# A graph attention layer on one core: more row buffers in the setup, self loops ahead of their states, stores moved in the round order

## The chip, the cores and the metric

The kernel runs on one core of a Trainium2 chip. The metric is device microseconds of one launch, from the first instruction to the last. The engines are named as in the profile: PE (matrix multiplies) with its weight loads PEld, DVE (vector), ACT (scalar, activation functions), POOL (the general engine, which here issues the gathers), and SP, which only issues transfers; SPq is SP's queue.

## The reference

12,500 nodes with 128 features, 400,000 edges sorted by destination, 32 features on an edge. One layer of a graph network:

```python
h   = relu(layernorm(x))
xl  = ln1(h) @ W_l ; xr = ln1(h) @ W_r          # 8 heads of 16
# every edge, and one self loop for each node with the mean edge feature
m   = leaky_relu(xl[src] + xr[dst] + ea @ W_e, 0.2)
a   = softmax over the edges of one dst of sum_c m[., h, c] * att[h, c]
g   = sum over the edges of one dst of a * xl[src] + bias
h2  = h + g
out = x + h2 + gelu(ln2(h2) @ W1 + b1) @ W2 + b2
```

## The kernel before, in words

**Setup (lines 704 to 745).** The 98 tiles of 128 nodes are taken in 25 quads. A loop over "rounds" r runs software-pipelined stages, each some rounds later than the one before: statistics of x on DVE (x_stats, L470), ReLU (L481) and squares (L506) on ACT, transposes and the product with W_l on PE, and x_l (L526) on DVE, which writes the row of 136 numbers that edges will fetch; x_l goes out to memory by SP (L534). x_l writes into one of only three tiles (L513), so the fourth x_l waits until the store of the first has landed.

In the same loop POOL fetches, by 24 x 4 indirect transfers (raw_gather, L268 to L276), rows of x for 24 of the 782 edge pairs; SP stores each group to memory three rounds later (raw_store, L279). The groups go through a ring of buffers (L269). The list rows_at (L719) says in which round a group is fetched. Three lumps of work stand in the loop too: edge_constants (L346, round 7, 22 operations on DVE), from_first (L387, round 12, which turns each edge's destination into a distance from the first one of its unit, and of its pair, with two big subtractions on POOL, L392, stored by SP, L398), and fits (L400, round 14, DVE, whose result `flag` decides which branch runs). At the end all engines go on to the branch; its pools begin with small memsets (POOL L876, DVE L878).

**Edge rounds (lines 1320 to 1339).** The 400,000 edges are 782 pairs of two units of 256 edges. One round handles a different pair in every stage; the number beside a stage is how many rounds after the pair's own round it runs. gather (-4) lets POOL issue four indirect transfers that fetch 128 rows each (L897); for the 24 prepared pairs it is one SP transfer instead (L892). windows (-3) lets SP load edge features and distances for four pairs (L908, L914) and the pair's window of xr (L918). place (-1, DVE L925) makes the one-hot matrix. combine (0, PE L939 to L943), slope (ACT L949) and bend (DVE L954) (1), score (2, PE L960, L961), lowest (DVE L968) and weigh (ACT L979) (3), turn (4, PE L987), keep_turned (5, ACT L992), collect (6, PE L1001), own_heads (7, DVE L1010, L1016), put (8, SP L1023, which writes a running state for the pair's nodes, one of two state arrays per unit). The ring of gathered rows has 12 buffers (L862): the gather of pair c needs the collect of pair c-12 to be over. Within an engine everything runs in the order of the program, and the order within a round is written by hand in the list `stages` (L1251), then `steps`, then `late_stages` (L1265), where windows and put stand.

**Node groups.** 25 groups of up to four node tiles are finished between the edge rounds when their edges are over. A group starts at its "round" and its 20 steps run in the offsets of the list `steps` (L1276): f_load (loads of both states, of xl and of xr, L1060), the self loop (f_order, f_z, f_bend, f_score, offsets 1 to 4), the softmax over two states and the self loop (f_low to f_h), the second norm, the two products with GELU between, and f_store (L1242), which adds three terms on DVE and issues the store of the result from SP in the same step (L1249). The last group starts at round 790, eight rounds after the last pair's own round. Groups start at least GAP = 23 rounds apart.

Of the kernel before, what the change touches and what calls it, by code (L numbers as in the profile page):

```python
# [13 lines left out]
F32 = mybir.dt.float32  # L14
BF16 = mybir.dt.bfloat16
I32 = mybir.dt.int32
AF = mybir.ActivationFunctionType
OP = mybir.AluOpType
# [3 lines left out]
P = 128  # L22
# [11 lines left out]
KU = 2  # L34
U = KU * P
UP = 2
QP = 4
RU = 14
# [10 lines left out]
AHEAD = 4  # L49
# [86 lines left out]
def tile_gnn(  # L136
# [23 lines left out]
    nc = tc.nc  # L160
# [8 lines left out]
    RP = -(-NU // RU)  # L169
    assert NU * U <= NCH * CE <= RP * RU * U  # L170
    x_t = x.rearrange("(t p) f -> p t f", p=P)
    out_t = out.rearrange("(t p) f -> p t f", p=P)
# [9 lines left out]
    dc_dram = dram.tile([RP * RU * U], BF16, name="dc_dram")  # L182
    du_dram = dram.tile([RP * RU * U], BF16, name="du_dram")
    raw = [{"c": c, "i": i, "round": r, "n": UP * KU} for i, (c, r) in enumerate(raw_pairs(NT, n_edges))]
# [36 lines left out]
    rng = pre.enter_context(tc.tile_pool(name="rng", bufs=1))  # L221
    node = pre.enter_context(tc.tile_pool(name="node", bufs=3))
# [8 lines left out]
    EP = RU * U  # L231
# [34 lines left out]
        )  # L266

    def raw_gather(d):  # L268
        d["x"] = node.tile([P, UP * KU, P], F32, name="raw", bufs=5)  # L269
        for j in range(d["n"]):  # L270
            nc.gpsimd.indirect_dma_start(  # L271
                out=d["x"][:, j, :],
                out_offset=None,
                in_=x,
                in_offset=bass.IndirectOffsetOnAxis(ap=src_raw[:, d["i"], j : j + 1], axis=0),
            )  # L276
# [97 lines left out]

    df = rng.tile([RP, EP + U + 1], F32, name="df")
    bad = rng.tile([RP, 2], F32, name="bad")

    def last_of_units():
        nc.vector.tensor_copy(lu, dc[:, U - 1 : EP : U])

        u = NUE - 1
        nc.sync.dma_start(
            lu[u // RU : u // RU + 1, u % RU : u % RU + 1],
            bass.AP(tensor=dst.tensor, offset=dst.offset + n_edges - 1, ap=[[0, 1], [1, 1]]),
        )

    def from_first():  # L387
        nc.vector.tensor_copy(df, dc)
        for step, to in ((U, du_dram), (UP * U, dc_dram)):
            de = df[:, 0:EP].rearrange("p (u e) -> p u e", e=step)  # L390
            dlb = rng.tile([RP, EP], BF16, name="dlb", bufs=2)
            nc.gpsimd.tensor_tensor(  # L392
                dlb.rearrange("p (u e) -> p u e", e=step),
                de,
                de[:, :, 0:1].to_broadcast([RP, EP // step, step]),
                op=OP.subtract,
            )
            nc.sync.dma_start(to.rearrange("(p e) -> p e", e=EP), dlb)  # L398

    def fits():  # L400
# [301 lines left out]
    LAST = 8  # L702
    first_xr = xr_steps(node, lambda: once_ps.tile([P, GN * P], F32, name="w_ps"))
    with tc.manual_schedule():
        make_identity(nc, ident)
        count_up()
        for t in xls:
            nc.gpsimd.memset(t[:, :, P:], 1.0)
        load_weights()
        load_x(0, min(GN, NT))  # L710
        load_raw()
        load_x(GN, min(3 * GN, NT - GN))
        for t in range(4 * GN, NT, 14):
            load_x(t, min(14, NT - t))
        load_dst()
        load_consts()
        nc.gpsimd.memset(empty, 0.0)
        nc.gpsimd.memset(empty[:, :, C + 1 : SH], CAP)
        rows_at = [i * 5 // 4 + (3 if i >= 10 else 0) for i in range(len(raw))]  # L719
        for r in range(max(max(len(qs), 9) + LAST + 1, rows_at[-1] + 4)):  # L720
            for d, at in zip(raw, rows_at):
                if r == at:
                    raw_gather(d)
                if r == at + 3:
                    raw_store(d)
            if r == 3:
                weights()
            if r == 7:
                edge_constants()
            if r == 8:  # L730
                last_of_units()
            if r == 12:
                from_first()
            if r == 14:
                fits()
            for t in slots(r - 2):
                nc.vector.reciprocal(t, t)
            for t in slots(r - 1):
                nc.scalar.activation(t, t, AF.Sqrt)
            for late, f in node_stages:  # L740
                if 0 <= r - late < len(qs):
                    f(qs[r - late], r)
            if 0 <= r - LAST < len(first_xr):
                first_xr[r - LAST](qs[0])
        clear(0)
# [82 lines left out]
def window_edges(  # L828
# [9 lines left out]
    nc = tc.nc  # L838
# [20 lines left out]
    with ExitStack() as es:  # L859
# [192 lines left out]
        def tiles(name, d, tag=None, bufs=1):  # L1052
            d[name] = fin.tile([P, GN, P], F32, name=f"f_{name}", tag=tag or f"f_{name}", bufs=bufs)
            return d[name][:, 0 : d["n"]]
# [2 lines left out]
            d[name] = ps2.tile([P, EPR], F32, name=ring)  # L1057
            return d[name]

        def f_load(d):  # L1060
            n, ts = d["n"], d["ts"]
            d["st"] = fin.tile([P, 2, GN, SW], F32, name="st", tag="big", bufs=3)
            for i in range(2):
                nc.sync.dma_start(d["st"][:, i, 0:n], state[i].rearrange("(t p h) f -> p t (h f)", p=P, h=H)[:, ts, :])
            d["xl"] = fin.tile([P, GN, XW], F32, name="f_xl")
            nc.sync.dma_start(d["xl"][:, 0:n], xl_t[:, ts, :])
            d["xr"] = fin.tile([P, GN, NS, P], BF16, name="f_xr")
            nc.sync.dma_start(d["xr"][:, 0:n], xs_t[:, ts, :, :])
# [137 lines left out]
        def f_up(k):  # L1206
            def up(d):
                n, u = d["n"], bank_of(d, f"u{k}")
                nc.tensor.matmul(  # L1209
                    u[:, 0 : n * P],  # L1210
                    w1_sb[:, k * P : (k + 1) * P],
                    d["hT"][:, 0:n].rearrange("p t f -> p (t f)"),
                    start=True,
                    stop=True,
                )

            return up

        def f_gelu(k):
            def gelu(d):  # L1220
                n = d["n"]
                if k == 0:
                    d["gel"] = fin.tile([P, 2, GN * P], F32, name="gel", tag="big", bufs=3)
                nc.scalar.activation(
                    d["gel"][:, k, 0 : n * P], d[f"u{k}"][:, 0 : n * P], AF.Gelu, bias=cols[:, 5 + k : 6 + k]
                )

            return gelu
# [12 lines left out]

        def f_store(d):  # L1242
            n = d["n"]
            y = tiles("yo", d, "f_b")
            up = d["y"][:, 0 : n * P].rearrange("p (t f) -> p t f", f=P)
            nc.vector.tensor_add(up, up, d["x"][:, 0:n])
            nc.vector.tensor_add(up, up, h_sb[:, d["ts"], :])
            nc.vector.tensor_add(y, up, b2_r[:, None, :].to_broadcast([P, n, P]))  # L1248
            nc.sync.dma_start(out_t[:, d["ts"], :], y)  # L1249

        stages = (  # L1251
            (-AHEAD, gather),
# [11 lines left out]
        )  # L1264
        late_stages = (  # L1265
            (-WAHEAD, windows),
            (LATE + 2, put),
        )
        sum_stages = (
            (0, sum_load),  # L1270
# [1 line left out]
            (3, mean),  # L1272
        )
        SUM_STEP = 2
        early = ((17, f_gelu(1)),)
        steps = (  # L1276
            (0, f_load),
            (1, f_order),
            (2, f_z),
            (3, f_bend),  # L1280
            (4, f_score),
            (5, f_low),
            (6, f_exp),
            (7, f_den),
            (8, f_out),
            (9, f_h),
            (10, f_stats),
            (11, f_root),
            (12, f_scale),
            (13, f_turn),  # L1290
            (14, f_turned),
            (15, f_up(0)),
            (16, f_up(1)),
            (16, f_gelu(0)),
            (18, f_down),
            (19, f_store),
        )
        GAP = 23
        last_round = n_pr + LATE + 2
        free = SUM_STEP * (NL - 1) + 5  # L1300
        for d, u in zip(groups, done_after(NT, n_edges)):
            d["round"] = max(free, (u // UP if u < NUE else n_pr) + LATE + 2)
            free = d["round"] + GAP
# [14 lines left out]

        CLEAR = 8
        with tc.manual_schedule():  # L1320
            for r in range(-AHEAD, max(last_round, groups[-1]["round"] + 20)):
                in_round(r, early)
                for late, f in stages:
                    c = r - late
                    if 0 <= c < n_pr:
                        f(c)
                for late, f in sum_stages:
                    i, off = divmod(r - late, SUM_STEP)
                    if off == 0 and 0 <= i < NL:
                        f(i)  # L1330
                if r > 0 and r % CLEAR == 0 and r // CLEAR < NT // GT:
                    clear(r // CLEAR)
                in_round(r, steps)
                in_round(r, enumerate(xr_steps), qs[1:])
                in_round(r, enumerate(raw_steps), raw)
                for late, f in late_stages:
                    c = r - late
                    if 0 <= c < n_pr:
                        f(c)
# [358 lines left out]
```

## Time and profile before

| what | value |
|---|---|
| median of three runs | 4033.95 us (4027.9 to 4034.51) |
| the profiled execution | 4031.16 us, span of its records 4029.0 us, clock granted 0.954 |
| busy: PE, DVE, ACT, POOL | 3542.0, 2539.1, 2131.2, 2980.9 us |
| instructions: PE, DVE, ACT, POOL | 19059, 5835, 4638, 3155 |
| chain that ended last, by engine | PE 38%, POOL 25%, DMA 22%, issue 13% |
| transfers | 560.85 MB, 139 GB/s in the mean |

A profile gives, for one execution, each engine's busy time and the groups of instructions with their mean duration and the idle time just before them, with the releaser: what ended that idle time. The timeline lists instructions in order: start, duration, engine, line, operation, and in square brackets the idle time before it and its releaser. A row can stand for several instructions in a stretch (x2, x13); its duration is then that of the stretch, waits included. "issue" is time in which the engine waited for nothing that is shown. A transfer's row on SPq is its issue; when it lands is seen only from what waits for it. The profiled execution's 4031.16 us is 2.16 us more than its span; the median of the runs is 2.8 us above the profiled execution.

### The profile page before, as it was taken

Reading aid. Unit: us, or ns where it says so; the run is one execution under the profiler, and the core shown is the slowest. Engines: PE = TensorE matmul, PEld = TensorE weight load, DVE = VectorE, ACT = ScalarE, POOL = GpSimd, SP = SyncE. Lnnn points to the kernel's source line nnn. Section 1 sums busy time; section 2 is a strip of 40 time slices with the busy share of each in tenths; the row PEclk is TensorE's granted clock in tenths of the full one; section 3 lists DMA queues with packets and bytes.
Section 4 is the critical chain, followed back from the end, with each engine's and each line's share of the span. In section 5 each row is a group of like instructions: output and inputs, shape, how many; then the busy total and the mean of one; then the engine's idle time right before and its main releaser. Section 6 shows DMA issues by size and latency. Waiting matters only on the chain.

```text
span 4029.0 us, 65580 instructions
## 1 busy us (share of the span) xinstructions
PE 3542.0 (88%) x19059; PEld 2507.7 (62%) x19255; DVE 2539.1 (63%) x5835; ACT 2131.2 (53%) x4638; POOL 2980.9 (74%) x3155
## 2 busy tenths in 40 slices
PE   3488888888899999999999999989999999989986
PEld 2356666666666666666666666666666666666664
DVE  6556666666666666666666666666666665656654
ACT  5544544544455555555465456555555555545553
POOL 6777777777777777777777777777777777777772
PEclk7799999999999999999999999999999999999998
DMA  6778878767666666656666666656666666566562
GB/s 185 207 175 192 193 184 190 174 160 168 164 120 137 124 124 132 125 112 131 131 126 131 126 132 124 128 127 115 124 136 126 125 131 130 111 131 112 120 133 56
DMA packets 646655, 560.85 MB, mean 139 GB/s; under 512 B 384830, under 2 KB 523949, under 8 KB 646045
## 3 DMA queue, kind: packets, MB, share of 16 engines
q1 hardware_dynamic: 545709, 339.00, 33.7%
q0 software_dynamic: 100000, 217.41, 30.4%
q8 instruction: 156, 2.56, 0.3%
q14 instruction: 214, 1.75, 0.2%
q10 hardware_dynamic: 576, 0.13, 0.0%
HBM read 489.80 MB, written 66.32 MB: 138 GB/s over the span
## 4 chain that ended last, share of the span: by engine, by line
PE 38%; POOL 25%; DMA 22%; issue 13%; SPq 1%; DVE 1%; ACT 0%; POOLq 0%; DVEq 0%; ACTq 0%
POOL xs L897 23%; DMA xs<-xl_dram,src_sb 21%; PE z L943 8%; PE acc L1001 8%; PE ab L961 7%; PE pt_ps L987 4%; PE z L939 4%; PE z L942 2%; POOL raw L271 2%; PE ab L960 1%; PE acc L1234 1%; PE acc L1209 1%; SPq L283 0%; DMA state<-rec 0%; DMA dc<-in_dst 0%
## 5 line engine op out<-in xcount | busy, mean ns | idle before, releaser
L897 POOL DMA_INDIRECT xs<-xl_dram,src_sb x3029 | 2868.9, 947 | 923.3 <-issue 792.7
L979 ACT ACTIVATE p<-ab,rec 128x256 f32<-128x256 f32 x1563 | 655.5, 471 | 1055.2 <-DVE rec L968 1039.1
L1010 DVE TENSOR_TENSOR own<-acc,diag 128x272 f32<-128x272 f32 x782 | 343.6, 439 | 1049.5 <-PE acc L1001 1034.9
L1001 PE MATMUL acc<-xs,pt 128*128 128x136 f32 x6250 | 879.8, 285 | 0.2 <-DVE f_yo L1248 0.2
L939 PE MATMUL z<-ident,xs 128*128 128x128 f32 x3125 | 562.6, 283 | 349.9 <-DMA xs<-xl_dram,src_sb 319.2
L939 PEld LDWEIGHTS z<-ident,xs 128*128 128x128 f32 x3125 | 398.7, 142 | 756.6 <-DMA xs<-xl_dram,src_sb 419.8
L943 PE MATMUL z<-ea,we_z 128*128 128x512 f32 x1564 | 839.4, 619 | 0.1
L961 PE MATMUL ab<-m,negrep 128*128 128x512 f32 x1564 | 799.5, 593 | 11.0 <-issue 1.1
L1001 PEld LDWEIGHTS acc<-xs,pt 128*128 128x128 f32 x6250 | 807.1, 196 | 0.4 <-PE pt_ps L987 0.4
L992 ACT COPY pt<-pt_ps 128x512 f32<-128x512 f32 x782 | 455.1, 582 | 619.5 <-PE pt_ps L987 613.8
L987 PEld LDWEIGHTS pt_ps<-ident,p 128*128 128x128 f32 x3125 | 408.6, 146 | 440.8 <-issue 391.2
L968 DVE TENSOR_REDUCE rec<-ab 128x2 f32<-128x512 f32 x781 | 539.7, 691 | 121.8 <-PE ab L961 113.3
L954 DVE TENSOR_TENSOR m<-z,zs 128x512 f32<-128x512 f32 x782 | 532.6, 681 | 127.4 <-ACT zs L949 127.0
L949 ACT ACTIVATE zs<-z 128x512 f32<-128x512 f32 x782 | 472.6, 604 | 41.1 <-DMA ea<-in_ea_t 32.2
L987 PE MATMUL pt_ps<-ident,p 128*128 128x128 f32 x3125 | 490.2, 281 | 1.9 <-ACT p L979 0.9
L1016 DVE TENSOR_REDUCE rec<-own 128x34 f32<-128x272 f32 x782 | 340.9, 436 | 26.7
L943 PEld LDWEIGHTS z<-ea,we_z 128*128 128x128 f32 x1564 | 308.0, 197 | 33.1
L961 PEld LDWEIGHTS ab<-m,negrep 128*128 128x128 f32 x1564 | 300.8, 192 | 37.4 <-issue 1.1
L942 PE MATMUL z<-ne,xrw 128*128 128x512 bf16 (+1 forms) x781 | 305.0, 391 | 0.2 <-issue 0.2
L925 DVE TENSOR_SCALAR ne<-dlw,nid 112x512 bf16<-112x512 bf16 x782 | 290.7, 372 | 14.0 <-DMA dlw<-du_dram 13.9
L960 PE MATMUL ab<-ne,farw 128*128 128x512 bf16 x588 | 225.4, 383 | 0.0
L271 POOL DMA_INDIRECT raw<-in_x,src_raw x96 | 95.6, 996 | 53.3 <-issue 28.5
(198 smaller groups left out, 2232.9 us busy)
## 6 DMA issues: line engine op xcount, KB each, us to landing
dlw<-dc_dram SPq DMA_DIRECT2D x196, 384.0 KB
ea<-in_ea_t SPq DMA_DIRECT2D x196, 256.0 KB
ea_s<-in_ea_t SPq DMA_DIRECT2D x98, 512.0 KB
xs<-xl_dram,src_sb POOLq DMA_INDIRECT x3029
state<-rec SPq DMA_DIRECT2D x1563, 9.0 KB
xrw<-xs_dram SPq DMA_DIRECT2D x782, 24.0 KB
state<-empty SPq DMA_DIRECT2D x28, 504.0 KB
st<-state SPq DMA_DIRECT2D x48, 288.0 KB
```

Of the source, the lines that this page charges most:

```text
L897: nc.gpsimd.indirect_dma_start(out=xs[:, j, :], out_offset=None, in_=xl_dram, in_offset=bass.IndirectOffsetOnAxis(ap=src_sb[:, c * KP + j ...
L939: nc.tensor.matmul(z[:, j * P : (j + 1) * P], d["xs"][:, j, 0:P], ident, start=(j == 0), stop=False, is_transpose=True)
L942: nc.tensor.matmul(z[:, :e], xrw[c % NV], d["ne"][:, :e], start=False, stop=False)
L943: nc.tensor.matmul(z[:, :e], we_z[:, c % QP, :], d["ea"][:, :e], start=False, stop=True)
L949: nc.scalar.activation(d["zs"][:, :e], d["z"][:, :e], AF.Copy, scale=SLOPE)
L954: nc.vector.tensor_tensor(d["m"][:, :e], d["z"][:, :e], d["zs"][:, :e], op=OP.max)
L961: nc.tensor.matmul(ab[:, :e], negrep.rearrange("p n h -> p (n h)"), d["m"][:, :e], start=False, stop=True)
L968: nc.vector.tensor_reduce(d["rec"][:, :, CX], d["ab"].rearrange("p (u e) -> p u e", e=U), AX.X, OP.min)
L979: nc.scalar.activation(d["p"][:, us], d["ab"][:, us], AF.Exp, bias=d["rec"][:, i, CX:SH], scale=-1.0)
L987: nc.tensor.transpose(d["pt_ps"][:, js], d["p"][:, js], ident)
L992: nc.scalar.copy(d["pt"][:, :e], d["pt_ps"][:, :e])
L1001: nc.tensor.matmul(d["acc"][:, i, :], d["pt"][:, j * P : (j + 1) * P], d["xs"][:, j, :], start=(j == js[0]), stop=(j == js[-1]),)
```

## The change

1. The ring of raw rows gets 12 buffers instead of 5, and rows_at loses its gap of three rounds.
2. The two subtractions leave POOL: from_first computes on DVE the negated first destination of each unit, and differ does the subtraction on ACT, in 7 rounds of three activations each (two of 256 columns, one of 512, on 112 partitions); keep_differences stores both at round 18. last_of_units is at round 9, from_first at 10, edge_constants at 13, fits at 15.
3. put runs at offset 7, in the round of own_heads, no longer one round later.
4. The node groups' steps are renumbered: the loads of xl and xr and the self loop up to f_bend run at offsets -4 to -1, before the states are loaded (f_state, offset 0); f_score follows at 1 and the rest three offsets earlier than before, so f_store is at 16. The store of the result is its own step, f_put, at 17. The last round is two earlier. The first groups' rounds move by two (201 for 199); from round 668 on all are the same.

```diff
-        d["x"] = node.tile([P, UP * KU, P], F32, name="raw", bufs=5)
+        d["x"] = node.tile([P, UP * KU, P], F32, name="raw", bufs=12)
...
     def from_first():
         nc.vector.tensor_copy(df, dc)
-        for step, to in ((U, du_dram), (UP * U, dc_dram)):
-            de = df[:, 0:EP].rearrange("p (u e) -> p u e", e=step)
-            dlb = rng.tile([RP, EP], BF16, name="dlb", bufs=2)
-            nc.gpsimd.tensor_tensor(
-                dlb.rearrange("p (u e) -> p u e", e=step),
-                de,
-                de[:, :, 0:1].to_broadcast([RP, EP // step, step]),
-                op=OP.subtract,
-            )
+        nc.vector.tensor_scalar(nf, df[:, 0:EP:U], -1.0, None, op0=OP.mult)
+
+    def differ(i):
+        for dlb, step, us in ((dlbs[0], U, range(UP * i, UP * i + UP)), (dlbs[1], UP * U, (i,))):
+            for u in us:
+                es = slice(u * step, (u + 1) * step)
+                f = u * step // U
+                nc.scalar.activation(dlb[:, es], df[:, es], AF.Identity, bias=nf[:, f : f + 1])
+
+    def keep_differences():
+        for dlb, to in zip(dlbs, (du_dram, dc_dram)):
             nc.sync.dma_start(to.rearrange("(p e) -> p e", e=EP), dlb)
...
-        rows_at = [i * 5 // 4 + (3 if i >= 10 else 0) for i in range(len(raw))]
-        for r in range(max(max(len(qs), 9) + LAST + 1, rows_at[-1] + 4)):
+        rows_at = [i * 5 // 4 for i in range(len(raw))]
+        for r in range(max(max(len(qs), 9) + LAST + 1, max(12 + RU // UP, 16), rows_at[-1] + 4)):
...
-            if r == 7:
+            if r == 9:
+                last_of_units()
+            if r == 10:
+                from_first()
+            if 0 <= r - 11 < RU // UP:
+                differ(r - 11)
+            if r == 11 + RU // UP:
+                keep_differences()
+            if r == 13:
                 edge_constants()
-            if r == 8:
-                last_of_units()
-            if r == 12:
-                from_first()
-            if r == 14:
+            if r == 15:
                 fits()
...
-        def f_load(d):
+        def f_state(d):
             n, ts = d["n"], d["ts"]
             d["st"] = fin.tile([P, 2, GN, SW], F32, name="st", tag="big", bufs=3)
             for i in range(2):
                 nc.sync.dma_start(d["st"][:, i, 0:n], state[i].rearrange("(t p h) f -> p t (h f)", p=P, h=H)[:, ts, :])
+
+        def f_load(d):
+            n, ts = d["n"], d["ts"]
             d["xl"] = fin.tile([P, GN, XW], F32, name="f_xl")
...
-            nc.sync.dma_start(out_t[:, d["ts"], :], y)
+
+        def f_put(d):
+            nc.sync.dma_start(out_t[:, d["ts"], :], d["out"])
...
-            (LATE + 2, put),
+            (LATE + 1, put),
...
-        early = ((17, f_gelu(1)),)
+        early = ((14, f_gelu(1)),)
         steps = (
-            (0, f_load), (1, f_order), (2, f_z), (3, f_bend), (4, f_score), (5, f_low), ...
+            (-4, f_load), (-3, f_order), (-2, f_z), (-1, f_bend), (0, f_state), (1, f_score), (2, f_low), ...
-            (18, f_down), (19, f_store),
+            (15, f_down), (16, f_store), (17, f_put),
         )
-        free = SUM_STEP * (NL - 1) + 5
+        free = SUM_STEP * (NL - 1) + 7
...
-            for r in range(-AHEAD, max(last_round, groups[-1]["round"] + 20)):
+            for r in range(-AHEAD, max(last_round, groups[-1]["round"] + 18)):
```

(In the list of steps one line here stands for several lines of the code.)

More of the change, by code (lines that the diff above doesn't have):

```diff
@@ L376, in tile_gnn @@
     bad = rng.tile([RP, 2], F32, name="bad")
+    nf = rng.tile([RP, RU], F32, name="nf")
+    dlbs = [rng.tile([RP, EP], BF16, name=f"dlb{i}") for i in range(2)]
     def last_of_units():
@@ L1243, in f_store @@
             n = d["n"]
-            y = tiles("yo", d, "f_b")
             up = d["y"][:, 0 : n * P].rearrange("p (t f) -> p t f", f=P)
+            y = d["out"] = tiles("yo", d, "f_b")
             nc.vector.tensor_add(up, up, d["x"][:, 0:n])
@@ L1274, in window_edges @@
         SUM_STEP = 2
-        early = ((17, f_gelu(1)),)
+        early = ((14, f_gelu(1)),)
         steps = (
[L1277 to L1296, printed above, removed]
+            (-4, f_load),
+            (-3, f_order),
+            (-2, f_z),
+            (-1, f_bend),
+            (0, f_state),
+            (1, f_score),
+            (2, f_low),
+            (3, f_exp),
+            (4, f_den),
+            (5, f_out),
+            (6, f_h),
+            (7, f_stats),
+            (8, f_root),
+            (9, f_scale),
+            (10, f_turn),
+            (11, f_turned),
+            (12, f_up(0)),
+            (13, f_up(1)),
+            (13, f_gelu(0)),
+            (15, f_down),
+            (16, f_store),
+            (17, f_put),
         )
```

## The prediction

> **What bounds the kernel now.** I read the table of groups first, then POOL's timeline, then the engines' timelines in the setup and in the last 70 us. In the page's table of groups (busy, mean ns, idle before):
>
> ```profile
> L897 POOL DMA_INDIRECT xs<-xl_dram,src_sb x3029 | 2868.9, 947 | 923.3 <-issue 792.7
> ```
>
> 2868.9 + 923.3 = 3792.2 us for 3029 gathers, 1.252 us each: 0.947 busy and 0.305 between two, and no single idle time in this group is over 0.3 us. POOL's timeline, cut to the rows that matter (start, duration, idle before and releaser):
>
> ```profile
> 30.22 0.94 POOL L271 DMA_INDIRECT raw<-in_x,src_raw  x1 [0.30 <-issue]
> 53.41 0.94 POOL L271 DMA_INDIRECT raw<-in_x,src_raw  x1 [22.25 <-DMA raw_dram<-raw]
> ...
> 63.39 2.72 POOL L271 DMA_INDIRECT raw<-in_x,src_raw  x1 [0.30 <-issue]
> 73.90 3.77 POOL L271 DMA_INDIRECT raw<-in_x,src_raw  x1 [0.30 <-issue]
> 82.69 12.28 POOL L392 TENSOR_TENSOR dlb<-df 112x3584 bf16<-112x3584 f32 x2
> ...
> 164.08 0.94 POOL L271 DMA_INDIRECT raw<-in_x,src_raw  x1 [0.30 <-issue]
> 167.44 0.93 POOL L876 MEMSET xrw<- 128x128 bf16 x6 [2.42 <-DMA raw<-in_x,src_raw]
> 168.53 0.95 POOL L897 DMA_INDIRECT xs<-xl_dram,src_sb  x1 [0.15 <-POOL xrw L876]
> ```
>
> The first edge gather starts at 168.53, the last ends at 3960.58: 3792.05 us without a gap. So PE at 88% is not the bound of the edge rounds; it waits for rows. The span is three pieces: setup 168.5, stream 3792.1, tail 68.4 (to 4029.0). I also paired each gather with the own_heads of the pair twelve before, which shows that its buffer is free: the nearest miss in the run is 8.2 us, the mean 17. The stream therefore changes only if its rounds fall a further 8 us behind. The change can act on setup and tail.
>
> **Setup, POOL.** 96 raw gathers start at 6.33 us at 1.248 us apart: 119.8 us if nothing stops them. Now 22.25 us go to the ring of five (the first store waits behind SP's loads) and 12.28 to L392. With twelve buffers group 12 is fetched at 6.33 + 60 = 66 us; the store it needs was issued at 41.02 and released POOL at 52.7, so no wait. Two gathers were stretched, by 1.78 and 2.83 us, beside DVE's L388 (2.16 us) and fits' L403 (3.88 us); both stay. POOL ends at 6.3 + 119.8 + 4.6 = 131 us instead of 165.0.
>
> **Setup, DVE, ACT, SP.** Then the node stages are late. From DVE's timeline:
>
> ```profile
> 39.38 0.27 DVE L348 COPY wer<-we_sb 128x128 f32<-128x128 f32 x1 [13.00 <-DMA we_sb<-in_w_e]
> ...
> 72.97 3.88 DVE L403 CUSTOM_DVE_ANT_0 junk<-df 112x3584 f32<-112x3584 f32 x1
> ...
> 83.56 11.96 DVE L585 TENSOR_TENSOR xr_parts<-xr,xr_parts 128x512 bf16<-128x512 f32 x1
> ...
> 100.60 1.12 DVE L526 SCALAR_TENSOR_TENSOR xl<-lr,roots_sb,bl_r 128x128 f32<-128x128 f32 x4 [2.82 <-DMA xl_dram<-xl]
> ...
> 151.88 0.61 DVE L526 SCALAR_TENSOR_TENSOR xl<-lr,roots_sb,bl_r 128x128 f32<-128x128 f32 x2 [1.16 <-DMA xl_dram<-xl]
> ```
>
> Round 7 loses 13.0 us there to a load and 5.4 to edge_constants; L585, a form that elsewhere takes about 0.7 us, takes 11.96 because it ran beside L392 and ended with it; SP stood behind L392 too, so an x_l waited 2.82. ACT sets the other rounds: 4 x 0.48 (ReLU) + 4 x 0.39 (squares) + half a copy of 0.56 + 0.1 = 3.86 us; the rounds from 111 to 127 us came 3.78 apart.
>
> New sum on DVE: round 7 begins at 26.2 as before; rounds 7 and 8 take it to 34. last_of_units waits for the destinations, which released SP at 36.3, so about 37; round 9 to 40.6. from_first, 2.2 + 0.2, and round 10: 46.5. In round 11 the fourth x_l, reached at 49, needs the landing of the first x_l store. SP does not come to that store before 51.6 (its first five raw stores run from 41.02 to 51.49 behind the loads), and a store then takes some 5 us (the x_l store issued at 95.41 released DVE at 100.60); some 16 more gathers of 64 KB are in those loads' way. I take 56.5, so 7.5 us of the 13 come back. Round 12 ends at 61.4, round 13 with edge_constants (5.4) at 69.7, round 14 at 73.2, round 15 with fits (72.97 to 79.70 before, so 6.7) at 83.4, round 16 at 87.2, round 17 at 91. Round 18 began at 108.8 before; from it to the last x_l took 152.5 - 108.8 = 43.7, so now 91.5 + 43.7 = 135.
>
> differ adds to ACT 7 x (2 x 0.39 + 0.57) = 9.5 us, by the spacing of two 128x256 activations of L979 (0.42, with a bias) and the 128x512 copy. Most of it lies in the time in which ACT waits anyway for DVE's two lumps of 5.4 and 6.7 us. The Trainium skill (ScalarE: Activation LUTs, What ACT_TABLE_LOAD costs) gives about 280 ns + 0.833 ns a column for an activation with a bias operand: 0.49 and 0.71, 7 x 1.69 = 11.8 us. The difference, 2.3 us, I keep as part of the range; uncovered, all of it would cost 9.5 to 11.8.
>
> A second rule speaks against the change. SBUF — State Buffer, Who interferes with whom: DVE and POOL share a port pair that one of them holds for a whole instruction. With POOL gathering all through the setup, edge_constants and every copy could stretch a gather; by the rule up to 5.4 us for edge_constants. The rows show stretches beside L388 and L403 only; beside L498's copies of 0.68 us, between 111 and 127 us, every gather has its 0.94. I take 0, and keep 5 in the range: POOL has some slack to the node stages' end anyway.
>
> The end of the setup: last x_l 135, its store issued by 136, landing some 2.5 later (a raw gather's last row landed 2.5 us after its start), memsets 1.1: first edge gather at 139.5, where POOL alone would allow 134.5. Gain 29 us; ends 22 (the store in round 11 lands 5 late and differ is uncovered in part) and 34 (POOL is the bound).
>
> **Edge rounds.** put now waits on SP for the own_heads of its own round, so SP loses a round of lead. Queued behind it are the next round's xrw, ea and dlw loads, and who waits for them is place (DVE) and combine (PE). At 2006.0 SP issued dlw for a pair whose place ran at 2020.4: 14.4 us ahead. One round of about 5 less leaves 9.4, and the first dlw of the run was used 7.2 us after its issue; so it costs nothing. In return the store of the result leaves its place in front of put: SP waited 228.3 us in 19 pieces at L1249 for f_yo, up to 31.3 at once, which the stream hid. f_state loads 2 rounds ahead of f_low, not 5: about 8 us are left after the put's landing, and a few us lost once in a group fit in the 8.2 us of the ring. f_load's and f_order's move costs nothing as POOL is late there. Bounds: 0 below, since POOL never waits now; above, 10 us. I take 0.
>
> **Tail.** The timeline of several engines at the end:
>
> ```profile
> 3959.64 0.94 POOL L897 DMA_INDIRECT xs<-xl_dram,src_sb  x1 [0.30 <-issue]
> ...
> 3977.74 0.39 SPq L1249 DMA_DIRECT2D out<-f_yo  x1
> ...
> 3978.33 10.13 SPq L1023 DMA_DIRECT2D state<-rec  x13
> ...
> 3989.57 1.00 SPq L1064 DMA_DIRECT2D st<-state  x2
> ...
> 3995.60 1.13 ACT L1073 COPY f_xo<-f_xl 128x512 f32<-128x512 f32 x1 [15.73 <-DMA f_xl<-xl_dram]
> ...
> 4001.70 0.19 DVE L1115 TENSOR_TENSOR f_mn<-f_mn,acc 128x32 f32<-128x32 f32 x1 [1.85 <-PE acc L1104]
> ```
>
> The previous group's result held SP until 3977.74; 13 puts stood behind it and came out 1.56 us a pair, though the last own_heads was over at 3982.9. Then the loads, and only with xl landed the self loop: 6.1 us to L1115. After it 27.3 us to the end stay as they are. Now: the previous group's last steps are three rounds earlier, which frees about 2 us of DVE and 3 of PE in the drain and makes the rounds before later; I count 1 us. put keeps pace and the last is out about 1 us after own_heads, at 3983 (5.5 earlier); the states' loads at 3984, landed 5.5 to 6 later, as xl's was 5 after its issue at 3990.62. f_load runs between puts at 3980.5, landed 3985.5, self loop ready 6.1 later at 3991.6; the states are there at 3990. So L1115 falls at about 3991 instead of 4001.7: gain 11 us, 7 to 13 (7 if puts pair by pair still pay 1.56 and xl lands late).
>
> **Sum.** Against the profiled execution: 4031.2 - 29 - 0 - 11 = 3991. The median is 2.8 above it, so 3994.
>
> **Rivals.** (A) The setup keeps more of its lateness: the loads of the first 50 us are what is late, x_l waits for them, and L392's work comes back on ACT. The gain in the setup is then 15 us, with 11 in the tail: 4008. For it: SP's queue is full until 51.5 and transfers hold more than all engines' mean share (1.05 to 1.14) from 10 to 35 us. Against: after 55 us the transfers' share is 0.2 to 0.6, and the big losses (L585, L392) are engine time. (B) The tail gives nothing because the states' landing was the last anyway, only 3 us: 4002. Against: L1114 had the states 2 us before L1115. (C) The other side: SP without its round of lead brings dlw late for every fourth pair. PE's mean is 3542/782 = 4.53 us in a round, the stream's 4.85; from 0.32 x 4 = 1.3 us late on, PE and not POOL sets the round, and at 1.5 us the 40 us are gone; at 2 us, 782 x 0.18 = 141: 4135. Against: 9.4 us of lead remain. (D) The clock or the ring eats it: no change, 4034.
>
> **How the numbers follow.** Forecast 0.72, A 0.14, B 0.07, C 0.03, D 0.04. Ends of the forecast: -34 - 13 = -47 gives 3987, -22 - 7 + 10 for the rounds gives 4015 at worst, though not all at once; with 6 us at the lower end for what I took as unchanged, 3981 to 4010. That takes in A and B. Under 0.2% (8 us) a measurement of this kernel can't tell from no change. Faster 0.93, same 0.04, slower 0.03.
>
> **What would show it.** First edge gather at 139 to 140, no idle over 0.3 in the raw gathers, L585 near 0.7, x_l's fourth waiting at about 49 to 56 us, the edge gathers still 3792 us, L1115 about 31 us after the last gather's end instead of 41. Wrong if the first gather stays after 155, or if edge gathers show idle times for PE's collect.

## The result, and the profile after

After the change the kernel takes 3999.89 us, the median of four runs (3998.34 to 4005.31); the kernel before took 4032.39 us in its four (4027.9 to 4034.51). The ratio is 0.9923, with a 95% interval from 0.9906 to 0.994: faster by some 24 to 38 us. The forecast was 3994, the range 3981 to 4010.

The profiled execution took 4000.49 us (4031.16 before), its span is 3998.7 us (4029.0), and the granted clock is 0.956 (0.954), so the difference of 30.3 us between the spans can be taken apart without a correction for the clock. Cut at the same two places as in the prediction, the start of the first edge gather and the end of the last:

| piece | before | after | measured change | predicted change |
|---|---|---|---|---|
| setup, to the first edge gather | 168.53 | 145.68 | -22.85 | -29 |
| stream of the 3029 edge gathers | 3792.05 | 3792.8 | +0.75 | 0 |
| tail, from the last gather's end | 68.4 | 60.2 | -8.2 | -11 |
| span | 4029.0 | 3998.7 | -30.3 | -40 |

**The stream.** The page's table of groups has this for the edge gathers of the kernel after (busy, mean ns, idle before):

```profile
L905 POOL DMA_INDIRECT xs<-xl_dram,src_sb x3029 | 2869.8, 947 | 923.1 <-issue 788.1
```

2869.8 + 923.1 = 3792.9 us for as many gathers of the same 947 ns. The stream still has no gap, and nothing that the change did to the rounds could show in it.

**The setup, on POOL.** POOL's timeline of the kernel after, cut to the rows that answer to those of before:

```profile
36.77 0.94 POOL L271 DMA_INDIRECT raw<-in_x,src_raw  x1 [0.95 <-DMA raw<-in_x,src_raw]
40.51 2.79 POOL L271 DMA_INDIRECT raw<-in_x,src_raw  x1 [0.30 <-issue]
52.79 0.94 POOL L271 DMA_INDIRECT raw<-in_x,src_raw  x1 [0.75 <-DMA raw<-in_x,src_raw]
65.50 1.20 POOL L271 DMA_INDIRECT raw<-in_x,src_raw  x1 [0.30 <-issue]
80.74 3.49 POOL L271 DMA_INDIRECT raw<-in_x,src_raw  x1 [0.30 <-issue]
131.97 0.94 POOL L271 DMA_INDIRECT raw<-in_x,src_raw  x1 [0.30 <-issue]
144.60 0.93 POOL L884 MEMSET xrw<- 128x128 bf16 x6 [11.69 <-DMA xl_dram<-xl]
145.68 0.95 POOL L905 DMA_INDIRECT xs<-xl_dram,src_sb  x1 [0.15 <-issue]
```

The wait of 22.25 us for the ring and the 12.28 us of subtractions are gone, and the raw gathers end at 132.91 instead of 165.0. They do not run without a stop, as the prediction had it: four of them wait between 0.54 and 0.95 us for the landing of an earlier raw gather (two are in the rows), which none did before, and lose 1.9 us by it. But now POOL stands idle for 11.69 us and is released by the landing of the last x_l store (xl_dram<-xl). Before, the row at this place had 2.42 us and a raw gather as its releaser. The engine that ended the setup has changed: it was POOL, and now it is the chain of the node stages.

**The setup, on DVE.** DVE's timeline of the kernel after, cut to the rows that matter:

```profile
37.65 0.17 DVE L381 COPY lu<-dc 112x14 int32<-112x14 int32 x1 [2.67 <-DMA dc<-in_dst]
60.53 1.13 DVE L530 SCALAR_TENSOR_TENSOR xl<-lr,roots_sb,bl_r 128x128 f32<-128x128 f32 x4 [10.97 <-DMA xl_dram<-xl]
78.92 0.68 DVE L589 TENSOR_TENSOR xr_parts<-xr,xr_parts 128x512 bf16<-128x512 f32 x1
79.51 3.90 DVE L407 CUSTOM_DVE_ANT_0 junk<-df 112x3584 f32<-112x3584 f32 x1
140.37 0.61 DVE L530 SCALAR_TENSOR_TENSOR xl<-lr,roots_sb,bl_r 128x128 f32<-128x128 f32 x2
```

L589 is the line that was L585: 0.68 us now, 11.96 before. The last x_l begins at 140.37, before at 151.88. Between them stands the new row that matters most: the fourth x_l waits 10.97 us for an x_l tile whose store is to land. DVE does no other work meanwhile. The windows of 50 to 60 us show it (PE, PEld, DVE, ACT and POOL busy with the number of instructions, then the clock, the transfers' share and GB/s), in the kernel after:

```profile
50.00:60.00 10.00, 0.86 (x6) 0.43 (x5) 0.00 (x0) 7.29 (x25) 7.19 (x8) 0.64 0.98 293
```

and in the kernel before:

```profile
50.00:60.00 10.00, 7.72 (x32) 6.35 (x32) 8.10 (x43) 9.63 (x43) 5.07 (x6) 0.50 0.44 142
```

DVE had 8.10 us of work in this stretch before and has none after, while the transfers went from 142 to 293 GB/s.

**The tail.** The timeline of several engines at the end of the kernel after, cut to the rows that matter:

```profile
3937.52 0.94 POOL L905 DMA_INDIRECT xs<-xl_dram,src_sb  x1 [0.30 <-PE z L947]
...
3944.91 0.39 SPq L1262 DMA_DIRECT2D out<-f_yo  x1
...
3956.93 0.43 SPq L1077 DMA_DIRECT2D f_xl<-xl_dram  x1
3957.41 0.50 SPq L1079 DMA_DIRECT2D f_xr<-xs_dram  x1
3958.16 0.36 SPq L1031 DMA_DIRECT2D state<-rec  x1
3958.36 0.30 DVE L1024 TENSOR_REDUCE rec<-own 128x17 f32<-128x136 f32 x1
3962.23 0.33 SPq L1031 DMA_DIRECT2D state<-rec  x1
3965.03 1.88 PE L1115 MATMUL acc<-negrep,f_m 128*128 128x8 f32 x8 [1.56 <-DVE f_m L1109]
3965.27 0.33 SPq L1031 DMA_DIRECT2D state<-rec  x1
3966.71 0.95 SPq L1072 DMA_DIRECT2D st<-state  x2
3970.92 0.22 DVE L1125 TENSOR_TENSOR f_mn<-st 128x32 f32<-128x32 f32 x1 [5.95 <-DMA st<-state]
3971.24 0.19 DVE L1126 TENSOR_TENSOR f_mn<-f_mn,acc 128x32 f32<-128x32 f32 x1
```

The reader should see three things. The previous group's result is out at 3944.91, long before the last own_heads (L1024) at 3958.36 to 3958.66; before, it held SP until after the drain had begun to pile up. The self loop's score (L1115) is over at 3966.91, before the states have landed, where it came last before. And yet the puts (L1031) of the last two pairs come out at 3962.23 and 3965.27, up to 6.6 us after the last own_heads.

### The profile page after: what moved, and what is told of

Same layout as the page of the kernel before. It is cut to its first block, busy times and chain, and to the rows that moved or that the text cites. A ratio compares the mean times of both kernels' runs of the same rounds, so it can differ in the third digit from the quotient of the medians.

```text
span 3998.7 us, 65597 instructions
## 1 busy us (share of the span) xinstructions
PE 3544.6 (89%) x19060; PEld 2514.3 (63%) x19255; DVE 2526.8 (63%) x5836; ACT 2143.9 (54%) x4659; POOL 2969.4 (74%) x3153
## 3 DMA queue, kind: packets, MB, share of 16 engines
q14 instruction: 213, 1.74, 0.2%
## 4 chain that ended last, share of the span: by engine, by line
PE 38%; DMA 23%; POOL 22%; issue 12%; DVE 0%; ACT 0%; POOLq 0%; SPq 0%; DVEq 0%; ACTq 0%
DMA xs<-xl_dram,src_sb 23%; POOL xs L905 22%; PE z L951 9%; PE acc L1009 8%; PE ab L969 7%; PE pt_ps L995 4%; PE z L947 4%; PE z L950 2%; PE ab L968 1%; PE acc L1245 1%; PE acc L1220 1%; PE pt_ps L573 0%; DMA state<-rec 0%; PE acc L1205 0%; PE acc L1098 0%
## 5 line engine op out<-in xcount | busy, mean ns | idle before, releaser
L905 POOL DMA_INDIRECT xs<-xl_dram,src_sb x3029 | 2869.8, 947 | 923.1 <-issue 788.1
L1024 DVE TENSOR_REDUCE rec<-own 128x34 f32<-128x272 f32 x782 | 340.9, 436 | 26.7
```

What stands on the lines that cost most here:

```text
L905: nc.gpsimd.indirect_dma_start(out=xs[:, j, :], out_offset=None, in_=xl_dram, in_offset=bass.IndirectOffsetOnAxis(ap=src_sb[:, c * KP + j ...
```

## Experiments

No kernel beyond these two was run. What follows about causes is therefore read from the two traces. It is argued from them; no run in which one part alone was undone or done alone has confirmed it. Three questions stay open, and each would be told apart by one edit that was not tried. The numbers in this list are estimates from the rows of the two traces.

1. Is the fourth x_l late because SP issues the first x_l store late, or because all transfers of the first 60 us are slow? That x_l was done at 34.91; SP came to its store at 54.13, behind five raw stores. Storing each raw group six rounds later, which puts all of them behind that x_l and for which the ring of 12 has room, would let SP issue it near 42. In the first case it has landed before the fourth x_l is reached at 49.5, the wait of 10.97 us goes, and the first edge gather comes up to 9 us sooner (no more, since POOL's raw gathers end at 132.91). In the second the store lands late all the same, and the first gather stays near 145.7. A fourth x_l tile alone would not tell the two apart, as the fifth x_l would then wait for the same store.
2. Are the puts of the last pairs slowed by f_load's loads? Putting f_load at offset -8 for -4 takes the loads away from these puts and changes otherwise only how long their tiles are held. If the loads are the cause, the span becomes some 2.5 to 4 us shorter (the two sizes are taken apart further on); if not, it stays.
3. How much does each half give by itself? The buffers and differ alone, without the move of put and of the self loop, and the reverse, would show whether the two gains add. The table of pieces suggests it, since the stream between them has not moved, but it doesn't prove it.

## Why the prediction was right, and where it was off

**The split of the span was right.** That POOL's stream is the bound of the rounds, that a change of the rounds therefore gives nothing there, and that setup and tail can be summed apart: measured 0.75 us for a forecast of 0. The ring's nearest miss, counted from the start of own_heads, is 10.0 us after the change and was 8.2 before. The rival in which SP loses its lead (C) did not come. These are SP's waits in the kernel after (line, releaser, total us, times, longest):

```profile
SPq L1031 <- DVE rec L1024: 770.0, 460, 10.3
SPq L1031 <- DMA state<-rec: 367.4, 225, 4.9
SPq L1262 <- DVE f_yo L1259: 77.2, 20, 24.6
```

The cost that was foreseen is really there: put's wait for own_heads went from 284.5 us in 182 pieces to 770.0 in 460. So is the return: the result's store waits 77.2 us instead of 228.3. Of what stands behind put in the queue, the dlw loads made DVE idle for 3.7 us in the whole run (13.9 before). Nearly all of that, 3.5 us, is the first load of the run. The lead was not what the prediction read: the load issued at 2006.0 is first used at 2023.56 (the place at 2020.4 is that of the pair before, which has the load before), so it led by 17.6 us and not 14.4. In the median over the run, from a dlw's issue to its first place, it went from 15.6 to 13.6 us, 2 us and not a round of 5. That was enough: the stream of gathers did not grow with the 485 us of additional waiting.

**The setup: right mechanism, one term too small.** The raw gathers end at 132.91 (foreseen 131), last_of_units begins at 37.65 (37), fits and the stages behind it take 6.75 us (6.7). From the end of that block, at 86.26, to the last x_l's end takes 54.7 us; the prediction's sum had 55.1 for it. The landing of the last x_l's store releases POOL 3.6 us after that x_l (3.4 foreseen). The raw gathers ended 2 us late for their own small waits, which cost nothing, as POOL then had 11.69 us to spare. What failed is the sentence on round 11: "In round 11 the fourth x_l, reached at 49, needs the landing of the first x_l store", priced with "I take 56.5". It was reached at 49.5 and ran at 60.53. SP's timeline of the kernel after shows why:

```profile
41.77 12.25 SPq L279 DMA_DIRECT2D raw_dram<-raw  x5
54.13 0.45 SPq L538 DMA_DIRECT2D xl_dram<-xl  x1
```

The five raw stores ahead of it take until 54.02, not 51.49 as before. So the x_l store starts 2.5 us later than the 51.6 that was taken from the trace of before, and lands about 6.4 us later instead of 5. Together that is the 4.0 us. The prediction took SP's times and a store's duration from a trace in which POOL stood still from 31 to 53 us, and named the additional gathers without a price for them. In the kernel after they run through that stretch: the transfers' share from 40 to 50 us is 1.04 (0.93 before), and from 50 to 60 us the 0.98 of the row above (0.44 before). That the gathers make the stores later is a coincidence in time and in size, and is not tested. It can hold for a part of the 2.5 us only. SP is 0.75 us late when it comes to the raw stores, and the issue of the first of them, whose data were long there, was slow without the gathers too. These are that store in the kernel after and in the kernel before:

```profile
41.77 5.80 SPq L279 DMA_DIRECT2D raw_dram<-raw  x1
```

```profile
41.02 4.56 SPq L279 DMA_DIRECT2D raw_dram<-raw  x1
```

At 41.02 in the kernel before, POOL had issued no gather for 10 us.

Some 2 us more were lost in rounds 12 to 14, so that fits began at 79.51 instead of 73.2. With both, 22.85 us came and not 29. That is near the lower of the ends named, 22, for which the prediction had a store landing 5 us late in round 11, and towards rival A, whose argument was just that the loads of the first 50 us are what is late; its gain of 15 was too small.

**What differ costs on ACT** was weighed between 9.5 us (a sum that takes 0.39 us where its text names 0.42; with that it is 9.9) and 11.8 us. Each round takes 1.51 to 1.53 us, as in these rows of ACT's timeline after:

```profile
55.76 1.53 ACT L398 ACTIVATE dlb<-df,nf 112x256 bf16<-112x256 f32 x3
63.97 0.21 ACT L747 ACTIVATE roots_sb<-roots_sb 128x8 f32<-128x8 f32 x1 [6.68 <-DVE roots_sb L476]
68.53 1.52 ACT L398 ACTIVATE dlb<-df,nf 112x256 bf16<-112x256 f32 x3
74.23 0.21 ACT L747 ACTIVATE roots_sb<-roots_sb 128x8 f32<-128x8 f32 x1 [4.18 <-DVE roots_sb L476]
```

Seven times 1.51 is 10.6 us, in the middle. A single one of them takes 0.49 to 0.51 us (256 columns) or 0.72 (512), within 0.02 us of what the prediction took from the Trainium skill (ScalarE: Activation LUTs, What ACT_TABLE_LOAD costs); they overlap a little, so that three of them, 1.70 to 1.74 us as a sum, take 1.51. The 11.8 us left this overlap out. And behind them ACT waits for DVE anyway, 6.68 and 4.18 us in the rows shown: these two rounds of differ lie in time that was free, as foreseen. The rule of the shared port, which the prediction set at 0 with 5 us kept in the range, cost next to nothing: beside edge_constants (66 to 71.7 us) one gather took 1.20 us, and those before and after it their 0.94. The 5.4 us of the prediction took the rule for every instruction of edge_constants; the Trainium skill (SBUF — State Buffer, Who interferes with whom) exempts some, reductions among them.

**The tail: the gain came, but not by the step that was to bring it.** "put keeps pace and the last is out about 1 us after own_heads" failed. The last put was over at 3965.60, 6.9 us after own_heads' end. Counted from the last gather's end that is +27.1 us, where before it was +27.9: the earlier put gave the tail 0.8 us. The drain ended 2 us sooner (1 foreseen), but the puts used most of that up: the states' load waits for the last put, and that came only 0.8 us earlier. The gain came from the other term: the self loop ran before the states instead of 6.1 us behind xl's landing. L1126 stands at +32.8 us, where L1115, the same step, stood at +41.1, and of these 8.3 us 7.6 lie between the last put's end and that step (5.64 us now, 13.24 before). From it to the end it is 27.46 us (27.3 before). The order of the last two arrivals is the reverse of the forecast: the score was ready at 3966.91, the states only at 3970.9. They landed 4.2 us after their issue, though, where 5.5 to 6 were taken, which hid part of the miss.

Why did the puts fall behind? Each pair's put waits for the landing of the one before it into the same state array. The first puts of the last three pairs are issued at 3958.16, 3962.23 and 3965.27: 4.07 and 3.04 us apart. These are their rows in the chain of work that ended last in the kernel after (start, then the time to the landing):

```profile
3958.16 3.96 DMA state<-rec
3962.23 2.92 DMA state<-rec
3965.27 1.42 DMA state<-rec
```

In the kernel before, the pairs of the backlog came faster. This is SP's timeline there, the first put of each pair, and a row of its chain that ended last:

```profile
3980.40 0.33 SPq L1023 DMA_DIRECT2D state<-rec  x1
3981.94 0.33 SPq L1023 DMA_DIRECT2D state<-rec  x1
3983.49 0.33 SPq L1023 DMA_DIRECT2D state<-rec  x1
3985.02 0.33 SPq L1023 DMA_DIRECT2D state<-rec  x1
```

```profile
3983.49 1.42 DMA state<-rec
```

That is 1.54 us a pair, of which 1.42 is the landing. So the 1 us of the forecast was too little in any case: in the kernel after the last three own_heads end within 1.5 us (3957.20 to 3958.66), and even at 1.54 us a pair from 3958.16 on the last put would have been over at 3961.57, 2.9 us behind. The excess over that is 4.07 - 1.54 + 3.04 - 1.54 = 4.0 us.

The only transfers that are new at this place are f_load's two, of 272 and 384 KB, issued at 3956.93 and 3957.41 just ahead of these puts. The windows of the kernel after show when they moved:

```profile
3958.00:3960.00 2.00, 0.00 (x0) 0.00 (x0) 0.63 (x3) 0.00 (x0) 0.00 (x0) 1.00 0.71 145
3960.00:3962.00 2.00, 0.99 (x4) 0.62 (x5) 0.00 (x0) 1.12 (x1) 0.00 (x0) 0.75 0.74 209
3962.00:3964.00 2.00, 1.46 (x12) 1.19 (x12) 0.00 (x0) 0.50 (x1) 0.00 (x0) 0.50 0.05 4
3964.00:3966.00 2.00, 0.97 (x5) 0.98 (x5) 0.75 (x1) 0.19 (x1) 0.00 (x0) 0.50 0.05 5
```

The first excess, 2.5 us, falls where the loads move; they would explain it. The second, 1.5 us, comes when they are over, at a share of 0.05; all that the trace shows there is that the issue of the same pair's other put, at 3962.77, took 1.60 us for the usual 0.33. Its cause stays open. Without both, the states would have been there at about the time of the score, 3966.91, and L1126 would stand near 3967.2, about 4 us sooner; the prediction's +31 would even have been passed. The sentence that is wrong by this reading is "f_load's and f_order's move costs nothing as POOL is late there". It holds for the rounds, and was not asked again for the drain, where POOL has nothing more to do and SP's small stores are on the path. That the loads hold the puts up, by the first excess, is an inference from the times; the second edit of the list would test it.

**Together.** The setup missed by 6.2 us, the tail by 2.8, the stream by 0.75: 9.7 us, which is the distance of the measured 30.3 from the 40 foreseen. The median came only 5.9 us above its forecast (3999.89 for 3994), and that is luck: the forecast had added 2.8 us, by which the profiled execution of before lay below its median, the profiled execution of after lies 0.6 above its own, and the distances of executions from spans differ by 0.4.

## What to carry to other kernels

Look for the engine whose stream has no gap, and cut the span into what lies ahead of it, the stream, and what lies behind: a wait that grew by 485 us inside the stream cost nothing here, and all of the gain came from the two ends. When a stall at an end is removed, what is next there should be priced with the traffic that the removal sets free; the old trace's durations may be too short. A load that is moved ahead so as to hide must be asked once more at the end of the run, where it may stand in front of small stores that wait for one another.

## What the runs showed of the hardware

A small store that waits for the one before it took 1.54 us a pair with little else under way. It took 4.07 us while 656 KB of loads from the same queue moved, and 3.04 us right after them. The issue of a 256 KB store held SP for 5.80 us at 41.77, at a transfers' share of 1.04 (40 to 50 us), and 4.56 us at the same place before, at 0.93, against 0.32 us for the one at 58.95. A gather was stretched by much only beside single long DVE instructions, 2.79 and 3.49 us beside the cast of 2.15 us and fits' 3.90 us; beside the many short ones of edge_constants, some 5.7 us in all, the longest took 1.20.
